# Whole expert blocks of batch 0 run beside batch 1's second pass, from a first list of their own

## The chip, the core and the metric

One core of a Trainium2 chip runs the kernel. The metric is device time in microseconds. TensorE (PE) multiplies matrices and transposes, VectorE (DVE) and ScalarE (ACT) work on tiles, GpSimd (POOL) issues indirect DMAs (gathers and scatters by a list of rows), SyncE (SP) issues plain DMAs. Each engine takes its instructions in order.

## What is computed

A block of a transformer on x of 2 batches x 4096 tokens x 512 features: linear attention, then a mixture of 8 experts of which each token uses 2. Six modulation vectors per batch (`sa, ca, ga, sb, cb, gb`) come from a condition.

```python
h = layernorm(x) * (1 + ca) + sa
q, k, v = split(h @ w_qkv.T); q, k = relu(q), relu(k)      # 16 heads of 32
vk  = einsum('bhen,bhdn->bhed', pad(v, 1), k)              # over all tokens of the batch
att = einsum('bhed,bhdn->bhen', vk, q); att = att[:-1] / (att[-1] + eps)
x = x + ga * (att @ w_proj.T + b_proj)
h = layernorm(x) * (1 + cb) + sb
logits = (h * rsqrt(mean(h*h)) * router_scale / sqrt(512)) @ router_logits
choices = top 2 of logits; weights = softmax over them
out[t] = sum over its 2 experts e: weight * scale[e] * ((gelu(h@Wg[e]) * (h@Wv[e])) @ Wl[e])
x = x + gb * out
```

All tiles are fp32.

## The kernel before, in words

Tokens are handled in blocks of 512 (four tiles of 128), eight per batch.

*First pass* (`prepare`, `first`): layer norm, transposes (`pt`, copied to `xT`), keys (`pk`), queries (`pq`, stored to `q_d`), and the sum of x times k over all tokens (`pa`, added into `acc`). Twelve steps per block, each a `yield`. It also makes sums of the experts' weights (`weight_sums`: `wraw` in, `wnew` out, 24 jobs) for the experts' seven-product scheme.

*Second pass* (`merge`, `attend`, `second_norm`, `route`): `merge` makes the batch's matrix `gm` from `acc` (`pks`, `pvk`, `pgm`). `attend` loads queries (`qi`) and x (`xb`), divides by the denominator (`qk`, `den`), transposes (`pqt`) and projects (`po`, L682). `second_norm` makes `h2`, which goes to DRAM (`h2_d`, `h_d` in the profile), and x so far goes to `out`. `route` takes the top two experts of one or two blocks' tokens, counts ranks with three matmuls into `prk`, and scatters token number and weight to `map_d` in DRAM by `slot` (L887, eight or sixteen scatters). Six steps per block.

*Lists*: when all tokens are routed, `ptot` (L983) sums the counts, and some 40 small VectorE steps make the list of `NBIG` = 25 whole blocks (512 tokens of one expert) and of small ones (128 tokens; `NSURE` = 29 always run, more under an `If`).

*Experts*: a whole block gathers its piece of the map (`mp`), its rows (`xg`) and weights (`wg` twice, `wl`; each a gather of plain quarters and one of the sums), transposes (`px`), and makes two gate matrices and a linear one with seven products each (`seven`, L1200; sums in `part` and `quar`). `put` scales by the batch's `gb` (chosen per token: `sel`, `gsel`) and adds the rows to `out` by a scatter (L1176). A put waits for the one before. Small blocks do the same with plain products (`pgs`, `py`).

The order is written out by generators, and Tile then places the instructions of each engine by their order and readiness. The part around the change:

```python
a, z = firsts(), seconds()
per_block = 3 * NT
for _ in range(NBLK * per_block):
    next(a)
for _ in range((NBLK - 1) * (NT + 2)):
    next(z)
    for _ in range(2):
        next(a, None)
for _ in a:
    pass
for _ in z:
    pass
```

So batch 0's first pass runs alone, then seven blocks of batch 0's second pass go beside batch 1's first, then what is left: batch 0's last block and all of batch 1's second pass, alone. All tiles of these passes lie in pools that are closed before the lists; the experts' pools open after. PSUM (eight banks) is split 2 `ps_t`, 2 `ps_m`, 2 x 2 `ps_w` in the passes, then 2 `pe_t`, 6 `pe_g`. In SBUF, five buffers `big` of 1 MB serve the passes; gate weights `wg` have three buffers, `wl` one.

Of the kernel before, what the change touches and what calls it, by code (L numbers as in the profile page):

```python
# [9 lines left out]
FP = mybir.dt.float32  # L10
# [23 lines left out]
NBIG = (NTOK * TOPK - E * (TB - 1) + TB - 1) // TB  # L34

# [15 lines left out]
def adaln_linear_attention_moe_kernel(  # L51
# [81 lines left out]
    with ExitStack() as st:  # L133
        wp = st.enter_context(tc.tile_pool(name="w", bufs=1))
        wk = st.enter_context(tc.tile_pool(name="wk", bufs=2))
        sm = st.enter_context(tc.tile_pool(name="sm", bufs=2))
        ps_t = st.enter_context(tc.tile_pool(name="ps_t", bufs=2, space=PSUM))
        ps_m = st.enter_context(tc.tile_pool(name="ps_m", bufs=2, space=PSUM))
        ps_w = st.enter_context(tc.tile_pool(name="ps_w", bufs=2, space=PSUM))

        def big(name):
            return wk.tile([P, KC, TB], FP, tag="big", name=name, bufs=5)

        def row(tag, name, bufs):
            return wk.tile([P, C], FP, tag=tag, name=name, bufs=bufs)

        def bank(name):
            return ps_m.tile([P, 512], FP, tag="mm", name=name)

        def two_banks(name):  # L150

            return ps_w.tile([P, 1024], FP, tag="m2", name=name)


        cnd = wp.tile([P, KC, B], FP, tag="cnd", name="cnd")
        nc.sync.dma_start(out=cnd, in_=cond)
        xin = {}

        def load_x(b, i):
            r0 = b * N + i * TB  # L160
            xt = wk.tile([P, NT, C], FP, tag="x", name=f"x_{b}_{i}", bufs=2)
            nc.sync.dma_start(
                out=xt, in_=x[r0 : r0 + TB, :].rearrange("(p t) c -> p t c", t=NT)
            )
            xin[(b, i)] = xt

        def chunks(src):
            return src.rearrange("(k p) n -> p k n", p=P)

        load_x(0, 0)  # L170
        wm_of = {}

        def load_mod(m):
            wm = big(f"wm_{m}")
            nc.sync.dma_start(out=wm, in_=chunks(wmod[:, m * C : (m + 1) * C]))
            wm_of[m] = wm
# [3 lines left out]
        wqk = [  # L180
            wp.tile([P, KC, 2 * C + E], FP, tag=f"wqk{b}", name=f"wqk_{b}") for b in range(B)
        ]
        raw = wqk[1]

        def load_raw(at, c0):
            nc.sync.dma_start(out=raw[:, :, at : at + C], in_=chunks(wqkv[:, c0 : c0 + C]))

        load_mod(0)
        load_mod(1)
        load_raw(0, C)  # L190
        load_mod(4)
        load_raw(C, 0)

        def small_in(name, shape, src):
            t = wp.tile(shape, FP, tag=name, name=name)
            nc.sync.dma_start(out=t, in_=src)
            return t

        rl = small_in("rl", [P, KC, E], rlog)
        rs = small_in("rs", [P, KC], rscale)  # L200
        load_x(0, 1)
        pes_sb = small_in("pes_sb", [P, E], pes.partition_broadcast(P))
        bpc = small_in("bpc", [P, KC], bprojc)
        brow = wk.tile([B, C], FP, tag="sq", name="brow", bufs=1)
        nc.sync.dma_start(out=brow, in_=bproj.partition_broadcast(B))

        nc.vector.tensor_scalar(rs, rs, float(C) ** -0.5, None, ALU.mult)
        nc.vector.tensor_tensor(rl, rl, rs.unsqueeze(2).to_broadcast([P, KC, E]), ALU.mult)


        silu = wp.tile([P, KC, B], FP, tag="silu", name="silu")
        nc.scalar.activation(silu, cnd, AF.Silu)

        modc = wp.tile([P, 5, KC, B], FP, tag="modc", name="modc")

        def mod_columns(m):
            wm = wm_of.pop(m)
            pc = bank(f"pmc_{m}")
            for g in range(KC):
                for k in range(KC):  # L220
                    nc.tensor.matmul(
                        pc[:, g * B : (g + 1) * B],
                        wm[:, k, g * P : (g + 1) * P],
                        silu[:, k, :],
                        start=(k == 0), stop=(k == KC - 1),
                    )
            nc.vector.tensor_scalar(
                modc[:, m].rearrange("p k b -> p (k b)"), pc[:, 0 : KC * B],
                float(m == 1), None, ALU.add,
            )  # L230

        rows_d = dram.tile([7, B * C], FP, tag="rowsd", name="rows_d")

        def keep_row(n, r):
            d = rows_d[n : n + 1, :]
            nc.sync.dma_start(out=d.rearrange("o (b c) -> (o b) c", b=B), in_=r)

        def spread(n, b, dst):

            d = rows_d[n : n + 1, b * C : (b + 1) * C]  # L240
            nc.sync.dma_start(out=dst, in_=d.partition_broadcast(P))

        GA, SB, CB, GB, BG, BK = range(6)

        def mod_row(m):
            wm = wm_of.pop(m)
            pm = bank(f"pm_{m}")
            for k in range(KC):
                nc.tensor.matmul(
                    pm[0:B, :], silu[:, k, :], wm[:, k, :],  # L250
                    start=(k == 0), stop=(k == KC - 1),
                )
            pr = pm[0:B, :]
            r = wk.tile([B, C], FP, tag="qi", name=f"modrow_{m}", bufs=4)
            if m in (2, 5):

                mag = wk.tile([B, C], FP, tag="qi", name=f"mag_{m}", bufs=4)
                nc.scalar.activation(mag, pr, AF.Abs)
                nc.vector.tensor_scalar(mag, mag, 0.25, None, ALU.max)
                nc.vector.tensor_scalar(r, pr, 0.0, 2.0, ALU.is_ge, ALU.mult)  # L260
                nc.vector.scalar_tensor_tensor(r, r, -1.0, mag, ALU.add, ALU.mult)
            else:
                nc.vector.tensor_scalar(r, pr, float(m == 4), None, ALU.add)
            keep_row(m - 2, r)
            if m < 5:
                pc = ps_t.tile([P, 512], FP, tag="tr", name=f"pmt_{m}")
                for k in range(KC):
                    nc.tensor.transpose(
                        pc[:, k * B : (k + 1) * B], r[:, k * P : (k + 1) * P], ident[0:B, 0:B]
                    )  # L270
                nc.vector.tensor_copy(
                    modc[:, m].rearrange("p k b -> p (k b)"), pc[:, 0 : KC * B]
                )
            return r

        def over_parts(cols, name):

            n = cols.shape[2]
            ps = bank(f"ps_{name}")
            for k in range(KC):  # L280
                nc.tensor.matmul(
                    ps[:, 0:n], ones, cols[:, k, :], start=(k == 0), stop=(k == KC - 1)
                )
            return ps[:, 0:n]

        def scaled(b, at):
            for k in range(KC):
                nc.vector.tensor_scalar(
                    wqk[b][:, k, at : at + C], raw[:, k, at : at + C],
                    modc[:, 1, k, b : b + 1], None, ALU.mult,  # L290
                )

        bias = {}

        def bias_row(n):

            pb = bank(f"pb_{n}")
            for k in range(KC):
                nc.tensor.matmul(
                    pb[0:B, :], modc[:, 0, k, :], raw[:, k, n * C : (n + 1) * C],  # L300
                    start=(k == 0), stop=(k == KC - 1),
                )
            r = wk.tile([B, C], FP, tag="qi", name=f"biasrow_{n}", bufs=4)
            nc.scalar.copy(r, pb[0:B, :])
            keep_row(BK + n, r)
            for b in range(B):
                bias[n, b] = wp.tile([P, C], FP, tag=f"bias{n}", name=f"bias{n}_{b}", bufs=2)
                spread(BK + n, b, bias[n, b])

        def over_j(a, n):  # L310
            return a.unsqueeze(3).to_broadcast([P, KC, B, n])

        def over_b(a):
            return a.unsqueeze(2).to_broadcast([P, KC, B, a.shape[2]])


        rlx = wp.tile([P, KC, B, EX], FP, tag="rlx", name="rlx")

        def router_columns():
            nc.vector.tensor_scalar(  # L320
                rlx[:, :, :, E], iota_e[:, 0:1].unsqueeze(2).to_broadcast([P, KC, B]),
# [12 lines left out]
            for b in range(B):  # L334
                nc.vector.tensor_copy(wqk[b][:, :, 2 * C :], rlx[:, :, b, 0:E])
# [45 lines left out]
        def later_rows():  # L381
# [7 lines left out]
            for b in range(B):  # L389
                spread(GB, b, gb[:, b])  # L390
# [1097 lines left out]
```

## Time and profile before

| | us |
|---|---|
| median of 3 runs | 2440.1 |
| lowest, highest | 2439.1, 2448.38 |
| the profiled execution | 2465.07 |
| its span, first to last instruction | 2463.3 |
| first pass of batch 0, `pk` from | 32.0 |
| second pass, `po` from and to | 451.4 to 1109.3 |
| `px` of the first whole block | 1148.8 |
| last product of a whole block | 2438 |

The profile is of one execution. A busy digit is the share of a slice in tenths; the slices are 61.6 us long. A row of the groups gives busy time, mean of one, and the idle time of the engine before it with what ended it. In a row of the table by stage, the columns are busy time and instructions of each engine, the granted TensorE clock, the share of the DMA engines and their rate.

### The profile page before, as it was taken

To read this page: it belongs to the slowest core of one execution; us is meant where nothing else is said; L and a number is where in the kernel's file an instruction comes from. 1 tells how busy PE (TensorE), PEld (TensorE's weight loads), DVE (VectorE), ACT (ScalarE), POOL (GpSimd) and SP (SyncE) were. 2 spreads that over 40 slices of the span, in tenths; PEclk is the share of its full clock that TensorE was granted. 3 is DMA by queue.
4 is the path that set the end of the run, shared out by engine and by line. 5 is a ranking of instruction groups with operands and counts; after the bars stand their busy time and mean duration, and the time that the engine had idled before them with its cause. 6 is when DMAs were issued, how large, how long until landed. Compare 5 with 4: busy or idle time off the path is not lost. (4 is left out here: it accounts for less than half of the span.)

```text
span 2463.3 us, 25420 instructions
## 1 busy us (share of the span) xinstructions
PE 2330.3 (95%) x9446; PEld 1688.4 (69%) x9446; DVE 1469.6 (60%) x2928; ACT 511.8 (21%) x1019; POOL 769.4 (31%) x723
## 2 busy tenths in 40 slices
PE   8999999999899998883899999999999999999996
PEld 4555565666566667662777778777887788877884
DVE  3475656666465648885565655655655566655663
ACT  1121111223232223442111111111111111111110
POOL 0110000000102022255544444444544445444431
PEclk9999999999899999996999999999999999999998
DMA  5685565233434336766777787777777777777763
GB/s 210 258 322 218 218 230 189 73 128 114 101 120 103 137 86 169 198 151 182 246 236 241 215 245 229 234 244 250 209 228 235 246 249 207 233 250 227 243 157 66
DMA packets 111729, 486.22 MB, mean 197 GB/s; under 512 B 18594, under 2 KB 18594, under 8 KB 77939
## 3 DMA queue, kind: packets, MB, share of 16 engines
q0 software_dynamic: 71584, 347.12, 45.3%
q1 hardware_dynamic: 40018, 137.44, 18.3%
q8 instruction: 76, 1.25, 0.2%
q14 instruction: 51, 0.41, 0.1%
HBM read 355.63 MB, written 128.88 MB: 197 GB/s over the span
## 5 line engine op out<-in xcount | busy, mean ns | idle before, releaser
L1200 PE MATMUL p_g<-xT,wg 128*128 128x256 f32 x1600 | 370.7, 380 | 0.0
L1200 PEld LDWEIGHTS p_g<-xT,wg 128*128 128x128 f32 x1600 | 302.5, 190 | 41.7 <-issue 1.9
L887 POOL DMA_INDIRECT map_d<-pair,slot x128 | 134.4, 1050 | 596.2 <-DVE slot L884 548.9
L1200 PE MATMUL p_g<-xS,wg 128*128 128x256 f32 x1200 | 283.6, 379 | 1.4 <-DVE xS L1272 1.4
L682 PE MATMUL po<-gm,qT 128*128 128x265 f32 (+1 forms) x1024 | 247.9, 394 | 13.1 <-issue 6.1
L1200 PEld LDWEIGHTS p_g<-xS,wg 128*128 128x128 f32 x1200 | 227.9, 190 | 32.8 <-DVE xS L1272 1.8
L517 PE MATMUL pq<-wqk,xT 128*128 128x264 f32 (+1 forms) x1024 | 233.0, 387 | 13.0 <-DVE den L658 13.0
L500 PE MATMUL pk<-wqk,xT 128*128 128x512 f32 x512 | 228.3, 593 | 2.8 <-DVE k L505 2.8
L537 PE MATMUL pa<-k,xh 128*128 128x512 f32 x512 | 227.2, 599 | 3.8 <-DVE acc L544 3.8
L517 PEld LDWEIGHTS pq<-wqk,xT 128*128 128x128 f32 x1024 | 196.6, 193 | 49.5 <-issue 18.1
L682 PEld LDWEIGHTS po<-gm,qT 128*128 128x128 f32 x1024 | 193.9, 195 | 50.3 <-issue 10.9
L1176 POOL DMA_INDIRECT out<-y_b,mp x100 | 158.1, 1581 | 180.1 <-DVE y_b L1173 157.3
L1354 PE MATMUL pgs<-wgs,xTs 128*128 128x512 f32 x464 | 205.6, 596 | 0.0
L1200 PE MATMUL p_l<-wl,aT 128*128 128x256 f32 x800 | 193.9, 379 | 0.0
L537 PEld LDWEIGHTS pa<-k,xh 128*128 128x128 f32 x512 | 98.1, 193 | 117.6 <-issue 111.8
L1354 PEld LDWEIGHTS pgs<-wgs,xTs 128*128 128x128 f32 x464 | 88.7, 191 | 111.7 <-issue 110.3
L500 PEld LDWEIGHTS pk<-wqk,xT 128*128 128x128 f32 x512 | 93.5, 190 | 104.4 <-issue 97.8
L1200 PEld LDWEIGHTS p_l<-wl,aT 128*128 128x128 f32 x800 | 147.9, 190 | 18.3 <-issue 0.5
L1113 POOL DMA_INDIRECT xg<-h_d,mp x129 | 131.9, 1022 | 72.7 <-issue 34.0
L1292 ACT ACTIVATE ge<-quar_g 128x512 f32<-128x512 f32 x100 | 62.9, 629 | 409.5 <-DVE quar_g L1208 395.0
L1200 PE MATMUL p_l<-wl,aS 128*128 128x256 f32 x600 | 141.7, 379 | 0.0
L1208 DVE TENSOR_TENSOR quar_g<-part_g,p_g 128x512 f32<-128x512 f32 x150 | 102.7, 685 | 53.6 <-PE p_g L1200 51.9
(267 smaller groups left out, 3017.3 us busy)
## 6 DMA issues: line engine op xcount, KB each, us to landing
x<-in_x SPq DMA_DIRECT2D x16, 1024.0 KB
q_d<-q SPq DMA_DIRECT2D x64, 256.0 KB
qi<-q_d SPq DMA_DIRECT2D x64, 256.0 KB
wraw<-in_wgate POOLq DMA_DIRECT2D x16, 1024.0 KB
xb_d<-x SPq DMA_DIRECT2D x16, 1024.0 KB
wgsum_d<-wnew POOLq DMA_DIRECT2D x16, 1024.0 KB
xb<-xb_d SPq DMA_DIRECT2D x16, 1024.0 KB
out<-xb SPq DMA_DIRECT2D x16, 1024.0 KB
```

What stands on the lines that cost most here:

```text
L500: nc.tensor.matmul(pk, xT[:, k, t * P : (t + 1) * P], w[:, k, 0:C], start=(k == 0), stop=(k == KC - 1),)
L517: nc.tensor.matmul(pq[:, C // 2 + c0 : C // 2 + c1], xT[:, k, t * P : (t + 1) * P], w[:, k, C + c0 : C + c1], start=(k == 0), stop=(k == K ...
L537: nc.tensor.matmul(pa, xh[t][:, g * P : (g + 1) * P], ks[t], start=(t == 0), stop=(t == NT - 1),)
L682: nc.tensor.matmul(po[:, C // 2 - EX + c0 : C // 2 - EX + c1], qT[:, g * P : (g + 1) * P], gm[:, g, c0:c1], start=(g == 0), stop=(g == KC ...
L887: ins = nc.gpsimd.indirect_dma_start(out=map_d, out_offset=IndirectOffsetOnAxis(ap=slot[:, k, t : t + 1], axis=0), in_=pair[:, k, t, :], i ...
L1113: return nc.gpsimd.indirect_dma_start(out=dst, out_offset=None, in_=src, in_offset=IndirectOffsetOnAxis(ap=ids, axis=0))
L1176: ins = nc.gpsimd.indirect_dma_start(out=out, out_offset=IndirectOffsetOnAxis(ap=token(mp, t), axis=0), in_=y, in_offset=None, compute_op= ...
L1200: nc.tensor.matmul(bank[:, c, :], left(s, c, k), rhs[:, k, :], start=(k == 0), stop=(k == KH - 1),)
L1208: nc.vector.tensor_tensor(r, one, two, ALU.add)
L1292: nc.scalar.activation(ge, g, AF.Gelu_apprx_tanh)
L1354: nc.tensor.matmul(p, xT[:, k, :], wg[:, :, quarters[k // KH], k % KH, :], start=(k == 0), stop=(k == KC - 1),)
```

## The change

- `NEARLY` = 9 whole blocks of batch 0's tokens (as many as its 8192 pairs are sure to fill) get a list as soon as batch 0 is routed (`early_lists`), with their nine map gathers at once. Their tokens are all of batch 0, so `put` uses `gb[:, 0]` as it is, and the sources and targets are `h2_d[0:N]` and `out[0:N]`.
- Batch 0's whole second pass now goes beside seven blocks of batch 1's first pass; the eighth follows with the early list.
- Blocks 0 to 7 are cut into steps and run beside batch 1's second pass. PSUM there is 2 transpose banks, one two-bank tile for `po`, 4 product banks.
- After it `late_lists` makes the lists of the other `NLATE` = 16 whole blocks and of the small ones; block 8 is issued after it. Then the 16 blocks run beside the 29 small ones, whose steps end seven steps before the last block does.
- Pools are ordered by how long their tiles live: what only the first pass uses (`at`, `ap`) on one side, what the second pass uses (`bp`, `bk`, `sm`) on the other; the experts' pool `ew` takes the first's place, the small blocks' `sw` the second's, waiting tile by tile. `big` is gone: `xT` has two buffers, weight sums and early loads two (`tmp`), `h2` one, and `wv`, `wo` share those of `xb`. `qo` has two instead of three, `bias` one (read again for batch 1), `wg` two.
- Routing takes blocks two at a time but the last two of each batch (before: the last four of all).

```diff
+NEARLY = (N * TOPK - E * (TB - 1) + TB - 1) // TB
+NLATE = NBIG - NEARLY
...
+        bias[n, b] = ap.tile([P, C], FP, tag=f"bias{n}", name=f"bias{n}_{b}")
+        spread(BK + n, b, bias[n, b])
...
+        alone = n % NBLK >= NBLK - 2
...
+    def early_lists():
+        with ExitStack() as st:
+            mt = pool(st, "mt_early", side="right")
+            n = whole_of(mt, totals("early"), "e")
+            ej, lj, used, _ = first_units(mt, n, NEARLY, "e")
+            place_whole(mt, ej, lj, 0, NEARLY, "e")
+            taken.append(used)
...
+            if early:
+                g = gb[:, 0]
...
-                out=out,
+                out=out[0:N, :] if early else out,
...
-        w = gw.tile([P, NRAW + NSUM, KH, QN], FP, tag="wg", name=f"wg_{j}_{m}", bufs=3)
+        w = ew.tile([P, NRAW + NSUM, KH, QN], FP, tag="wg", name=f"wg_{j}_{m}", bufs=2)
...
+    def block(j):
+
+        more = j + 1 < NBIG
+
+        soon = more and j + 1 != NEARLY
+        if more:
+            fetch_big_rows(j + 1)
+        yield from gate_big(j, 0)
+        if more:
+            fetch_gate(j + 1, 0)
+        yield
+        yield from gate_big(j, 1)
+        if more:
+            fetch_gate(j + 1, 1)
+        if NEARLY <= j + 1 and j + 2 < NBIG:
+            fetch_big_map(j + 2)
+        yield
+        if soon:
+            turn_big(j + 1)
+        yield
+        yield from linear_big(j)
+        if more:
+            fetch_lin(j + 1)
+        if more and not soon:
+            turn_big(j + 1)
+        yield
...
+    def second_passes():
+        yield from seconds(0)
+        early_lists()
+        for j in range(NEARLY):
+            fetch_big_map(j)
...
+    in_turn(a, per_batch - 3 * NT, second_passes(), (NBLK + 1) * (NT + 2) + 1)
...
+    z = seconds(1)
+    next(z)
+    st_a.close()
+    st_p.close()
+    ew = pool(ctx, "ew")
...
+    psum["t"] = pool(st_p, "ps_t2", 2, space=PSUM)
+    psum["w"] = pool(st_p, "ps_w2", 1, space=PSUM)
+    psum["g"] = pool(st_p, "ps_g2", 4, space=PSUM)
...
+    in_turn(blocks(0, NEARLY - 1), STEPS * (NEARLY - 1), z, (NBLK + 1) * (NT + 2) - 1)
+    st_b.close()
+    mt_late = pool(ctx, "mt_late", side="right")
+    late_lists(mt_late)
+    sw = pool(ctx, "sw", side="right")
+    fetch_big_map(NEARLY)
+    fetch_big_map(NEARLY + 1)
+    fetch_small(0)
+    for _ in block(NEARLY - 1):
+        pass
...
+    in_turn(
+        blocks(NEARLY, NBIG), STEPS * NLATE - STEPS // 3, smalls(NSURE), 2 * (NSURE + 1)
+    )
```

`in_turn(one, n, other, m)` takes a step of `one`, then as many of `other` as keep both in proportion, and at the end drains `other`, then `one`.

## The prediction

> **What bounds the kernel now.** I read the page's table of slices first, then busy time by stage, then the timeline of TensorE where the stages meet, then the waits of that stretch.
>
> ```profile
> span 2463.3 us, 25420 instructions
> PE 2330.3 (95%) x9446; PEld 1688.4 (69%) x9446; DVE 1469.6 (60%) x2928; ACT 511.8 (21%) x1019; POOL 769.4 (31%) x723
> PE   8999999999899998883899999999999999999996
> PEclk9999999999899999996999999999999999999998
> ```
>
> TensorE is the bound almost everywhere; one hole lies in slices 16 to 20. By stage:
>
> ```profile
> core 0: us, PE busy (x) PEld busy (x) DVE busy (x) ACT busy (x) POOL busy (x), PEclk, DMA share, GB/s
> 427.00:910.00 483.00, 469.02 (x1749) 310.36 (x1749) 276.90 (x602) 129.56 (x284) 49.88 (x48) 0.98 0.36 110
> 926.70:1112.30 185.60, 154.21 (x723) 126.58 (x721) 159.54 (x500) 86.04 (x194) 68.51 (x64) 0.94 0.70 176
> 1112.30:1148.80 36.50, 2.22 (x11) 2.04 (x12) 22.14 (x107) 5.61 (x13) 23.19 (x29) 0.54 0.48 113
> 1148.80:1200.00 51.20, 41.14 (x162) 30.56 (x162) 18.22 (x28) 9.44 (x15) 26.77 (x29) 0.86 0.82 292
> 1200.00:2441.00 1241.00, 1241.00 (x5367) 964.84 (x5366) 742.35 (x1232) 201.19 (x349) 564.38 (x483) 1.00 0.74 225
> ```
>
> The first row is batch 1's first pass beside batch 0's second. The next is batch 1's second pass alone: VectorE is busy 86% and TensorE starves. Then come routing, lists and first fetches. The last row, the experts, has no TensorE idle time at all.
>
> ```profile
> 824.63 0.60 PE L670 MATMUL pqt<-ident,qi 128*128 128x128 f32 x4
> 825.07 3.69 PE L682 MATMUL po<-gm,qT 128*128 128x265 f32 x16
> 828.59 7.18 PE L517 MATMUL pq<-wqk,xT 128*128 128x256 f32 x32
> 1121.07 0.57 PE L983 MATMUL ptot<-cum,ones 128*128 128x8 f32 x2
> 1148.77 1.39 PE L1263 MATMUL px<-ident,xg 128*128 128x128 f32 x4 [27.12 <-DMA xg<-h_d,mp]
> 1203.70 1.89 PE L1200 MATMUL p_l<-wl,aT 128*128 128x256 f32 x8
> 1205.42 1.89 PE L1200 MATMUL p_l<-wl,aS 128*128 128x256 f32 x8
> ```
>
> Costs at full rate are read from start to start: a second-pass tile is 0.44 us of transposes and 3.52 of `po`; a product of a whole block is 1.73.
>
> **A rule against the row.** By busy time the lone second pass loses 185.6 - 154.2 = 31 us. The Trainium skill (Perfetto Trace Analysis, Identifying the Most-Contended Engine) says that matmul occupancy is a poor measure, because matmuls are pipelined. Here the row does hold stretched matmuls (clock 0.94), so I count: 32 tiles x 3.96 = 126.7, merge 8.2 (`pvk` 3.7, `pgm` 4.5), rank products 3.6, together 138.5. The loss is 47 us, and I take it; the row would give 16 less.
>
> Lost now: 47 alone, 35.5 of the 36.5 until the first rows land, and in 1148.8 to 1200 what remains after 14 products (24.2), 3.5 of transposes and 6.9 of the first small block's `pgs`: 16.6. **Together 99 us.** This is all that covering can win; the matmuls do not change.
>
> **The change, part by part.**
>
> *Whole blocks 0 to 7 beside batch 1's second pass.* One block is 21 products x 1.727 + 16 transposes x 0.11 = 38.0 us; eight are 304. The second pass adds 126.7 and about 3 of rank products: TensorE 434 us. VectorE: the expert stage uses 742.35/1241 x 49.3 = 29.5 us per 49.3 us cycle (start of `py` to start of `py`). Off go 1.16 small blocks of 2.3 us and the block's four `gsel` and `sel` (3.2 by their rows), which early blocks do not make: 23.6. Eight are 189, with the second pass's 159.5 this is 348 us, 80% of 434. DMA: the lone pass used 0.70 x 185.6 / 8 = 16.2 us of all engines per block; a whole block takes 64% of the expert stage's bytes (7.6 MB against 3.7 for a small one), so 0.74 x 1241 x 0.64 / 25 = 23.5. Sum 39.7 of 54.2 us, 73%: the share at which the expert stage has no stall. So TensorE bounds the mixed stage. Its loss can't be read from before; below stands 0 (expert stage), above the 17% of the lone pass's row (31.4/185.6), 74 us. The stage is nearer in VectorE load to the first mixed row (57%, 2.9% idle) than to the lone one: I take 4%, 18 us.
>
> *PSUM and weights.* Four product banks instead of six and one two-bank tile instead of two give VectorE about two products, 3.5 us, of lateness; gate weights have two buffers instead of three. A gather starts when its old half is done and is needed about 26 us of products later, 36 with the second pass's share; 1.84 MB at 225 GB/s fly 8.2 us. Nothing, under that cover; without it 8 us per gather.
>
> *Merge of batch 1.* Today other blocks' `po` lie around `pvk` and `pgm`; idle there is only 1.5 + 2.2 + 0.7 us. Now the first pass has just ended and only block 0's transposes can fill: 6 us (0 to 15, the upper end if row fetches wait for old tiles too).
>
> *Early list, nine map gathers.* Some 20 VectorE steps of about 0.25 us, the scatters of the last route (8 x 1.26 on POOL) and 9 x 1.25 us of gathers, all emitted before the last first-pass block, 43 us of TensorE. Nothing; uncovered about 30.
>
> *Late list beside block 8.* Today the last route's first step starts at 1116.65 and the transposes at 1148.77: 32.1 us. POOL is moved past more: second map, small weights, small map and row, 5 x 1.25, and 3.9 for the map to land before its rows. VectorE shares the time with block 8. So 42 us or more against 36.3 us of products: 10 us lost (0 if the route runs ahead, 25 if block 8's steps go first). What is late next is the first weight gather of block 9, behind those rows.
>
> *Late stage.* Sixteen blocks and 29 small ones: 608 + 29 x 11.2 = 932 us of TensorE. DMA and POOL per us of TensorE stay as now (1.81 small ones per 58 us block instead of 1.16 per 51). Nothing.
>
> *Tail.* Today `py` and its put follow the last whole product: 3.6 us of `py` and a put that waits for the block's four. The small ones now end seven steps earlier: 5 us saved.
>
> *Memory by life.* Weight sums have two buffers of their own, the `h2` tile one, `qo` two, each bias one. Three sums per 43 us block take 3 x (2.7 us of VectorE + 1 MB in and 1 MB out); a q tile is stored in about 4 us and 7 are there. Nothing, with 0 to 15 us kept for the range; at the turn to batch 1 the bias reload stands behind the store of `xb_d` on SP, two `pk` banks (6.9 us) cover it. The one large stall of the first mixed stage, 11.3 us at 637 (VectorE behind a late `qi` load), I leave in.
>
> **Does a busy VectorE slow the gathers?** The rows of the lone pass and of the expert stage:
>
> ```profile
> L887 POOL DMA_INDIRECT map_d<-pair,slot x64: 952/961/1823, 963.2 to 1109.1; - x64
> L1113 POOL DMA_INDIRECT wg<-wgsum_d,wrow x40: 933/937/1013, 1279.0 to 2269.2; - x40
> ```
>
> The Trainium skill (SBUF — State Buffer, A bandwidth-pool intuition that's wrong) tells of a gather's issue of about 620 ns that takes 3100 beside a VectorE copy, since both want one port pair. With VectorE 86% busy the median is 961 ns against 937 at 60%. By the row the 14 issues per block stay near 20 us; by the rule, five times, they would be some 70 us in a 54 us block and POOL the bound. The row decides.
>
> **Sum.** 99 - 18 - 6 - 10 + 5 = 70 us. The profiled execution took 2465.07 us (span 2463.3), 25 more than the median of 2440.1; I take the same 70 off: 2370, and a span near 2393. 0.5%, about what a measurement of this kernel can tell, is 12 us.
>
> **Rivals.**
>
> *Lock-step, 0.20.* VectorE's order is fixed. Today it waits 269/25 = 10.8 us per block for products (its `part` and `quar` rows). If second-pass work can't fill those waits, a block costs 23.6 + 10.8 + 159.5/8 = 54.3 us, exactly TensorE's 54.2; each wait for one then delays the other. Five us more per block are 40: 2410. For it: 76.5 us of VectorE waiting for `qi` loads today, one of which stopped TensorE. Against: the first mixed row hides nearly all of them.
>
> *POOL behind the scatters, 0.08, slower.* POOL is one queue in order, and its scatters wait for `slot`: 548.9 us in all, 22.4 at a time in the lone pass, then 16 x 1.26 = 20 us of issue. Nothing stands behind them now; weight gathers will. Their slack is 36 - 8 = 28 us. If a route's scatters stand in the queue half a mixed block (27 us) ahead of their slots, they hold it for 27 + 20 = 47, TensorE stops for 19, five routes cost 95: 2465. It decides from a hold of 28 us, and is slower than before from some 45. Against: the queue was ordered by what is expected ready, so gathers should go first.
>
> *It does not start early, 0.04.* If the new tiles must wait for all of the first pass's (old stores too), block 0 starts some 15 us late: 2385. Whole-tensor waits between early gathers and `h2` stores would follow program order, no more than a few us per block.
>
> **Numbers.** Forecast 0.68, its own range 2345 to 2395. Range 2335 (mixed stage without loss, late list covered) to 2422 (lock-step with a little more). Faster 0.88 (forecast, most of lock-step, late start), same 0.04, slower 0.08.
>
> **What would show it.** Right: TensorE 9 in nearly all slices, clock 1.0 in the mixed stage, `px` no longer waiting 27 us for rows, VectorE near 80% there, a loss of some 10 us once before the late stage. Wrong: idle TensorE in the mixed stage released by VectorE (lock-step) or by weight gathers behind `map_d` scatters on POOL, or a first pass longer than now.

## The result, and the profile after

The changed kernel took 2409.5 us (median of 4 runs) beside 2441.9 for the one before: ratio 0.986, interval 0.983 to 0.989. It is 32 us faster, where 70 were forecast. The kernel before takes 2442 to 2448 us on some chips and about 2460 on others, and the changed kernel reacts to this more strongly than the one before; so each comparison below is of times on one chip, and the text says what the kernel before took there.

The page of the changed kernel (busy times, then tenths of 40 slices):

```profile
span 2406.8 us, 25334 instructions
PE 2323.5 (97%) x9448; PEld 1683.3 (70%) x9448; DVE 1450.5 (60%) x2915; ACT 536.4 (22%) x1040; POOL 766.8 (32%) x726
PE   7999899999999999999999989999999999999996
PEclk9999999999999999999999999999999999999998
```

The hole of slices 16 to 20 is gone. Busy time by stage: batch 0's first pass, the first overlapped stage, the mixed stage, the change to the late stage, the late stage:

```profile
core 0: us, PE busy (x) PEld busy (x) DVE busy (x) ACT busy (x) POOL busy (x), PEclk, DMA share, GB/s
165.00:425.00 260.00, 240.21 (x764) 141.31 (x763) 147.02 (x254) 43.66 (x91) 20.99 (x39) 0.97 0.64 230
460.50:944.10 483.60, 476.25 (x1818) 319.17 (x1817) 298.63 (x710) 141.51 (x311) 84.06 (x84) 1.00 0.41 128
954.40:1366.20 411.80, 404.86 (x1991) 352.31 (x1989) 326.88 (x715) 146.51 (x274) 172.45 (x149) 1.00 0.68 201
1366.20:1477.60 111.40, 99.97 (x457) 85.21 (x457) 77.70 (x199) 25.80 (x44) 63.30 (x62) 0.94 0.66 203
1477.60:2384.00 906.40, 906.40 (x3739) 667.91 (x3738) 492.86 (x817) 145.51 (x254) 409.00 (x355) 1.00 0.76 238
```

The third row is what was forecast: TensorE 98% busy, VectorE 79%, clock 1.00. The first row is the surprise: the first pass has 20 us of idle TensorE, where the same 260 us of the kernel before read

```profile
165.00:425.00 260.00, 258.19 (x852) 153.95 (x850) 154.56 (x266) 47.60 (x101) 18.06 (x34) 1.00 0.62 222
```

with nearly as many bytes moved. Busy time hides stretched matmuls, so losses below are counted as in the prediction: from start to start, less the cost at full rate. For a pair profiled on one chip (kernel before 2442.7 us, changed kernel 2412.0):

| stage, us lost by TensorE | before | after |
|---|---|---|
| until 165 us | 14.5 | 16.4 |
| rest of batch 0's first pass | 2.1 | 27.2 |
| first overlapped stage | 24.2 | 17.0 |
| merge of batch 1 | 2.5 | 4.4 |
| batch 1's second pass (after: beside blocks 0 to 7) | 26.3 | 12.2 |
| lists and change to the next experts | 52.5 | 17.5 |
| the rest | 2.3 | 1.3 |
| sum | 124.4 | 96.0 |

Sums differ by 28.4, times by 30.7. From the merge to the next experts 47 us less are lost, and 25 of them are paid back in batch 0's first pass, which the change was not thought to touch.

### The profile page after: what moved, and what is told of

It reads as the page before. It is cut to its first block, busy times and chain, and to the rows that moved or that the text cites. A ratio compares the mean times of both kernels' runs of the same rounds, so it can differ in the third digit from the quotient of the medians.

```text
span 2406.8 us, 25334 instructions
## 1 busy us (share of the span) xinstructions
PE 2323.5 (97%) x9448; PEld 1683.3 (70%) x9448; DVE 1450.5 (60%) x2915; ACT 536.4 (22%) x1040; POOL 766.8 (32%) x726
## 3 DMA queue, kind: packets, MB, share of 16 engines
q1 hardware_dynamic: 40018, 137.44, 17.5%
## 5 line engine op out<-in xcount | busy, mean ns | idle before, releaser
L914 POOL DMA_INDIRECT map_d<-pair,slot x128 | 129.1, 1008 | 464.9 <-DVE slot L911 428.2
L542 PE MATMUL pq<-wqk,xT 128*128 128x264 f32 (+1 forms) x1024 | 244.0, 397 | 19.4 <-ACT xl L551 15.1
L709 PE MATMUL po<-gm,qT 128*128 128x265 f32 (+1 forms) x1024 | 237.4, 383 | 5.4 <-DVE den L685 4.6
L1215 POOL DMA_INDIRECT out<-y_b,mp x100 | 163.6, 1636 | 143.7 <-DVE y_b L1212 116.0
L1239 PEld LDWEIGHTS p_l<-wl,aS 128*128 128x128 f32 x600 | 114.5, 192 | 16.8 <-issue 1.4
```

Of the source, the lines that this page charges most:

```text
L542: nc.tensor.matmul(pq[:, C // 2 + c0 : C // 2 + c1], xT[:, k, t * P : (t + 1) * P], w[:, k, C + c0 : C + c1], start=(k == 0), stop=(k == K ...
L709: nc.tensor.matmul(po[:, C // 2 - EX + c0 : C // 2 - EX + c1], qT[:, g * P : (g + 1) * P], gm[:, g, c0:c1], start=(g == 0), stop=(g == KC ...
L914: ins = nc.gpsimd.indirect_dma_start(out=map_d, out_offset=IndirectOffsetOnAxis(ap=slot[:, k, t : t + 1], axis=0), in_=pair[:, k, t, :], i ...
L1215: ins = nc.gpsimd.indirect_dma_start(out=out[0:N, :] if early else out, out_offset=IndirectOffsetOnAxis(ap=token(mp, t), axis=0), in_=y, i ...
L1239: nc.tensor.matmul(bank[:, c, :], left(s, c, k), rhs[:, k, :], start=(k == 0), stop=(k == KH - 1),)
```

## The experiments

Two questions stood after the first profile: whether the 25 us of the first pass come from memory by life, or from the lists or the order; and whether what lies between 2465 (the profile of before) and 2440 (its median) is one odd execution, the profile itself, or something else. Each expectation below has its own letters for its theories.

**The kernel before again**, for the second question. 

> The kernel before, unchanged, profiled once more. Its profile shown with the prediction took 2465 us, 25 more than the median of its other runs, while the changed kernel's profile took what its other runs took. Theory A: that one execution lost some 25 us more than usual, so part of the 99 us that I counted as lost was never there to win in the median; a new profile then spans some 2440 and is shorter in one or two places that can be named (the 11 us stop near 637 us in the first mixed stage, or the lone second pass). Theory B: a profile costs this kernel 25 us each time; then the new span is near 2463 again with the same losses by stage.


It took 2462.6, with the losses of the first profile (144.9 in all against 147.1), while 39 runs of it there had a median of 2459.7. So neither an odd execution nor the cost of a profile: on that chip the kernel is that slow.

**Memory by life alone**, in the kernel before:

```diff
-            return wk.tile([P, KC, TB], FP, tag="big", name=name, bufs=5)
+            tag, bufs = "tmp", 2
+            if name.startswith("xT_"):
+                tag = "xT"
+            elif name.startswith(("h2_", "hk_")) or name == "wm_4":
+                tag, bufs = "h2", 1
+            elif name.startswith(("wv_", "wo_")) or name in ("wm_2", "wm_3"):
+                tag = "xb"
+            return wk.tile([P, KC, TB], FP, tag=tag, name=name, bufs=bufs)
...
-                qt = row("qo", f"q_{b}_{i}_{t}", 3)
+                qt = row("qo", f"q_{b}_{i}_{t}", 2)
```

> The kernel before with the smaller buffers of the change alone: xT its own two, weight sums and early loads two (tmp), h2 one, wv and wo those of xb, qo two instead of three. Order, lists and experts as before. Theory A (the first pass lost its buffers): some 20 us slower than before, 2460, with TensorE idle time between 175 and 400 us as in the changed kernel (29 us there by my count of matmuls against starts, none before). Theory B (that idle time comes from the new order of the changed kernel): within 5 us of before.


2494.5 beside 2459.7, ratio 1.014 (1.012 to 1.016): 35 us slower, where some 20 were expected. The first pass after 165 us lost 28.0 us (0.2 in the kernel before there). Its row:

```profile
165.00:425.00 260.00, 242.57 (x779) 142.91 (x778) 147.49 (x255) 44.13 (x92) 20.99 (x39) 0.97 0.64 229
```

This is the changed kernel's row, to 3 us in every column. What VectorE waits for there, first in the kernel before, then with the memory by life:

```profile
DVE acc L544 <- PE pa L537: 49.0, 24, 2.7
DVE q L523 <- PE pq L517: 34.7, 18, 2.9
DVE bn L469 <- DMA x<-in_x: 1.0, 1, 1.0
```

```profile
DVE q L530 <- DMA q_d<-q: 20.3, 3, 7.6
DVE wnew L453 <- DMA wraw<-in_wgate: 19.3, 9, 3.7
DVE bn L476 <- DMA x<-in_x: 14.1, 5, 4.3
DVE wnew L453 <- DMA wraw<-in_wlin: 10.6, 4, 7.0
```

VectorE waited for TensorE before; now it waits for DMAs as well, and since its order is fixed, TensorE's operands stand behind these waits. Theory A holds: the smaller buffers alone bring the loss. The next three runs ask which buffer it is.

**A third `qo` buffer** in the changed kernel (`ga` moves into the buffers of `qk` to make room):

```diff
-            qt = row("qo", f"q_{b}_{i}_{t}", 2, ap)
+            qt = row("qo", f"q_{b}_{i}_{t}", 3, ap)
...
-        ga = row("ga", f"ga_{b}", 1)
+        ga = row("qk", f"ga_{b}", 2)
```

> The changed kernel with a third buffer for qo, as before (ga takes one of the two qk buffers to make room). In the changed kernel VectorE waits 20 us for stores of q between 175 and 425 us, 13 us of TensorE idle time behind it. Theory A1 (qo is the narrow one): 10 to 15 us faster than the changed kernel, some 2397. Theory A2 (the two buffers of the weight sums are, and the q waits only follow from them): less than 5 us, some 2406.


2462.4 beside 2459.7 for the kernel before; the changed kernel itself, in a later run on this chip, took 2464.0. The waits for `q_d` were gone, but those for `x` (16.9 us) stayed, those for raw weights rose (22.6 to 36.5), and the first pass still lost 24 us. Not `qo`.

**The sums two at a time over 12 blocks**, in the changed kernel:

```diff
-            for _ in range(3 * E // NBLK):
-                next(wsums, None)
-            yield from steps
+            for m, _ in enumerate(steps):
+                if m in (0, 6):
+                    next(wsums, None)
+                yield
```

> The changed kernel with the 24 weight sums spread: two jobs per first-pass block, one before its first step and one before its seventh, over twelve blocks, instead of three at the start of each of eight. Buffers as in the change. Theory A2 (VectorE stops in its order for weights that come late through two buffers): the waits of wnew for wraw (22 us) go, batch 0's first pass is 15 to 25 us shorter, 2390. Theory A1 (qo): 5 us or less, 2405.


2456.5, beside the same 2459.7. Loads of raw weights still followed each other every 13.3 us (12.9 in the changed kernel), and the first pass still lost 24 us: the edit hardly moved the loads, so that it tells little.

**Raw weights into the idle `xb` buffers**:

```diff
-            raw = temp(f"wraw_{n}")
+            raw = temp(f"wraw_{n}", 1)
```

> The changed kernel, with the raw weights of the sums read into the two xb buffers, which nobody uses in batch 0's first pass; the two tmp buffers keep the sums alone. Theory A (the chain load, sum, store through two buffers holds VectorE, and TensorE behind it): the first pass of batch 0 loses under 8 us instead of 21 to 29, 18 to 25 us faster than the changed kernel. Rival (all the loads of this stage queue for the same DMA engines, as the third qo buffer suggests): over 15 us still lost there, the time within 6 us of the changed kernel.


2476.7, against 2463.8 for the changed kernel there: 13 us slower, a miss. More buffers did free the chain: a sum every 8.0 us, all loads issued by 285 us. But until then transfers filled the DMA engines to 84% (the last number but one of this row):

```profile
165.00:290.00 125.00, 104.27 (x325) 60.63 (x326) 84.47 (x147) 19.76 (x41) 16.43 (x31) 0.92 0.84 311
```

In the whole stage VectorE waited 29.7 us for `x`, and the loss stayed 29 us. So more buffers for the sums do not bring the time back.

**The common turn.** In the kernel before, the sums shared five `big` buffers with `xT`, one after the other in turn, so that a sum had to wait for a tile of the block it was in. The timelines of POOL and SP show it: once settled, a raw load is issued 6.9 us after each `x` load, and no other within 12 us of it. In the changed kernel, from 143 to 323 us, two lie around each, 10 to 12 us ahead and 0 to 3 behind, and from 170 to 323 the `x` loads come 50 to 52 us apart and not 43. So, with no byte more:

```diff
-            return a0.tile([P, KC, TB], FP, tag="tmp", name=name, bufs=2)
+            return a0.tile([P, KC, TB], FP, tag="tmp", name=name, bufs=4)
...
-        xT = a0.tile([P, KC, TB], FP, tag="xT", name=f"xT_{b}_{i}", bufs=2)
+        xT = temp(f"xT_{b}_{i}")
```

> The changed kernel with xT back in the pool of the weight sums' buffers, four that turn in common in place of two and two; no byte of memory more. Theory A2 (what the change lost is the common turn, in which a sum had to wait for the block's own tiles, so that its transfers fell between the x loads): the first pass of batch 0 loses under 8 us instead of 26, VectorE waits for x under 5 us there, and the time is 18 to 25 us below the changed kernel. Rival (four buffers are too few for both, the fifth was what mattered): over 15 us still lost, within 8 us of the changed kernel either way.


2399.0 beside a kernel before at 2448.2: ratio 0.980 (0.976 to 0.984). The first pass after 165 us lost 4.5 us, and its `x` loads come 43 to 44 us apart again. The places are not those of the kernel before: one raw load is still 2 to 3 us behind an `x` load, but from 262 us on the next ones lie 14 us or more away on either side. Again, beside the changed kernel itself:

> The changed kernel with the common turn of xT and the sums' buffers, now beside the changed kernel itself. Theory A2: 20 to 25 us below it, whatever the conditions, the loss of batch 0's first pass under 8 us against 20 to 29. Rival (the 2399 came from conditions without disturbed bursts): within 8 us of it.


2444.2 against 2464.0 for the changed kernel and 2461.6 for the one before. The turn is worth 20 us where 20 to 25 were expected; the loss there went from 28.8 to 6.5. Its row of the stage, and three of its waits:

```profile
165.00:425.00 260.00, 254.77 (x849) 152.30 (x849) 150.58 (x263) 48.85 (x103) 19.73 (x37) 1.00 0.63 225
```

```profile
DVE wnew L471 <- DMA wraw<-in_wlin: 26.8, 6, 6.2
DVE bn L494 <- DMA x<-in_x: 4.6, 1, 4.6
DVE q L548 <- DMA q_d<-q: 3.5, 1, 3.5
```

`qo` still has two buffers, and its 20 us of waits are nearly gone. The waits for raw weights are not: 34.3 us in all, about what the run with the third `qo` buffer had (36.5), which lost 24 us; beside that run it is the wait for `x` that is gone (16.9 to 4.6). That separate buffers bring the loss and a common turn takes most of it away is shown. How it acts is not tested by itself: by the place of the transfers, or by their pace, since in the common turn raw loads come every 14.1 us (14.4 in the kernel before, 12.9 in the changed one), about three a block.

**The changed kernel elsewhere.** 

> The changed kernel itself, beside the kernel before at about 2459. Theory (the scatters' bursts cost TensorE 8 to 18 us each in these conditions, in every version): 2455 to 2465, ratio 0.998 to 1.002, and TensorE loses 40 to 50 us in the mixed stage, nearly all of it in the three stretches where 16 map_d scatters follow each other. Rival (the variants tried so far carry costs of their own, the change is worth its 32 us everywhere): about 2427, ratio 0.987, mixed stage losing under 15 us.


2463.8 beside 2462.1: ratio 1.0005 (0.999 to 1.002). The 32 us were gone. A second time, on another chip:

> The changed kernel once more, as the measure for the three below. It took 2409 beside a kernel before at 2442, and 2464 beside one at 2462. If what hampered it there belongs to those conditions, it loses under 15 us in the mixed stage wherever the kernel before takes about 2448 or less, and stands at 2410 to 2430; where the kernel before takes about 2460, it stands at 2460 again.


2464.0 beside 2461.6. The mixed stage lost 57 and 53 us in these two, and 10 in the first profile. Its row in the second:

```profile
972.20:1426.80 454.60, 421.96 (x1991) 359.76 (x1989) 327.38 (x715) 146.97 (x274) 173.25 (x149) 0.95 0.61 182
```

The engines do the same work as in the first profile and take 43 us more for it. TensorE behind a burst of 16 map scatters (a burst: scatters of `route` one after the other on POOL), in that run:

```profile
1146.68 0.81 PE L1239 MATMUL p_g<-xS,wg 128*128 128x256 f32 x3
1148.50 0.59 PE L1239 MATMUL p_g<-xS,wg 128*128 128x256 f32 x2 [1.01 <-issue]
1149.90 0.38 PE L1239 MATMUL p_g<-xS,wg 128*128 128x256 f32 x1 [0.81 <-issue]
1150.62 0.78 PE L1239 MATMUL p_g<-xS,wg 128*128 128x256 f32 x1 [0.34 <-issue]
1152.73 0.58 PE L1239 MATMUL p_g<-xS,wg 128*128 128x256 f32 x1 [1.33 <-issue]
1154.83 2.62 PE L1239 MATMUL p_g<-xT,wg 128*128 128x256 f32 x4 [1.52 <-issue]
```

Matmuls of one product, waiting for nothing that the profile shows, come one by one. The same place in the first profile of the changed kernel:

```profile
1137.72 3.62 PE L1239 MATMUL p_g<-xT,wg 128*128 128x256 f32 x16
1141.17 1.89 PE L1239 MATMUL p_g<-xS,wg 128*128 128x256 f32 x8
1142.90 1.89 PE L1239 MATMUL p_g<-xT,wg 128*128 128x256 f32 x8
```

From a burst's start to 14 us past its end, three bursts of batch 1 cost 12.7, 11.0 and 14.7 us in the one, 1.5, 0.1 and 0.1 in the other. The burst of 8 that follows them cost 0.1 us or less in both.

**Every block routed alone** (8 scatters in a row and not 16), in both kernels:

```diff
-        alone = n % NBLK >= NBLK - 2
+        alone = True
...
-            alone = n >= len(order) - 4
+            alone = True
```

The first two lines are of the changed kernel, the others of the one before.

> The changed kernel with every block routed alone, so that its map scatters go out 8 at a time and not 16. In the runs so far 16 in a row cost TensorE 4 to 15 us, 8 in a row under 1 us unless something else waits there too. Theory B (it is the length of the burst): the stretches behind the scatters of batch 1 lose under 3 us each instead of 10 to 13, and 30 to 40 us fall off the changed kernel, to about 2425. Rival (it is the number of scatters, or their place beside other loads): the same loss in twice as many pieces, and the doubled small steps on VectorE on top, 0 to 10 us slower than the changed kernel.

> The same edit in the kernel before, which lost 9 to 13 us behind each burst of 16 in its lone second pass. Theory B: 25 to 35 us faster than the kernel before; the changed kernel with the edit is then as far below this one as in the first comparison, 15 to 35 us. Rival (the number of scatters): within 8 us of the kernel before, or slower, since VectorE is the busy one in the lone second pass and gets more steps.


2444.5 and 2462.5 beside 2448.2: with the edit the changed kernel is 4 us below the kernel before as it was, and the kernel before loses 14 us by it. (The changed kernel without the edit was not run on this chip.) Behind the bursts of the mixed stage TensorE lost 1.1 us or less, as expected, but the stage lost 32 us all the same, in other places. With the common turn as well:

> Both of these edits in the changed kernel. If both theories hold the gains add: 50 to 60 us below the changed kernel, about 2405 in these conditions, and the fastest of all. If only the bursts matter, as the routed-alone kernel; if neither, within 10 us of the changed kernel.


2432.8, 34 us slower than the common turn alone: the mixed stage lost 27.5 us against 12.8, the first overlapped stage with the merge 35.0 against 21.2. Where bursts cost little, twice as many small steps and bursts only add. As the common turn alone had no long losses behind its bursts there (at most 2.4 in the mixed stage), whether routing alone helps where 16 in a row hurt stays untested; for it speaks that on the two chips of about 2460 the burst of 8 behind the mixed stage's three cost 0.1 us or less.

**Every scatter twice**, with the common turn:

```diff
-        for k in range(TOPK):
+        for k in (0, 1, 0, 1):
```

> The common turn, and each of the 128 map scatters sent twice (the same values to the same rows). If small scatters in long rows hold up all engines' issue: 10 us or more lost behind each of the bursts of batch 1, now 32 and 16 in a row, 40 us or more on the whole. If only POOL and its queue feel them (128 x 1.27 us = 163 us of issue, which other weight gathers stand behind): 8 to 30 us slower, TensorE waiting for gathers and not in issue. If neither: within 5 us.


2579.2 against 2444.2: 135 us slower, far beyond the 40. What TensorE waits for from 950 to 1500 us, longest first:

```profile
PE px L1306 <- ACT xT L1309: 33.3, 5, 31.3
PE po L709 <- issue: 21.0, 13, 3.2
PE p_g L1239 <- issue: 16.3, 15, 1.6
```

Batch 1's bursts of 32 lost 26 to 36 us each, and no weight gather is in this list. The burst of 8 that had cost 0.1 us on this chip is one of 16 now, and cost 11. Behind the first burst of 32 the other engines stand without a wait too:

```profile
1200.20 0.69 DVE L715 TENSOR_TENSOR xb<-po,xb 128x512 f32<-128x512 f32 x1 [17.11 <-issue]
1201.05 0.72 ACT L722 ACTIVATE sv<-xb,lm 128x512 f32<-128x512 f32 x1 [24.09 <-issue]
```

The scatters are the cause. By what way they hold the engines, and why the same bursts cost so much more on one chip than on another, stays open; no run tells whether the recording of the profile has a part in it.

**Without the overlap**: the second pass emitted whole, blocks 0 to 7 behind it.

```diff
-    in_turn(blocks(0, NEARLY - 1), STEPS * (NEARLY - 1), z, (NBLK + 1) * (NT + 2) - 1)
+    for _ in z:
+        pass
+    for _ in blocks(0, NEARLY - 1):
+        pass
```

> The changed kernel without the overlap: the rest of batch 1's second pass is emitted whole, and blocks 0 to 7 behind it; lists, memory and the late stage stay as changed. The overlap's worth by the prediction's own steps is 47 (lone second pass) less 18 (mixed stage), 29 us: 29 us slower than the changed kernel, with VectorE above 80% in a lone second pass again. Rival (the bursts cost the same wherever they lie, so that most of the 47 stays in the mixed stage): within 12 us of the changed kernel.


2482.9 against 2463.8: the overlap is worth 19 us there, between the two forecasts, and VectorE is busy 74% in the lone pass, not above 80. The lone pass lost 72 us, 46 of them behind its three bursts of 16; the mixed stage lost 57, 36 of them behind the same three. Most of what a burst costs stays under the overlap.

**Two blocks beside the late list**, first alone, then with the common turn:

```diff
-    in_turn(blocks(0, NEARLY - 1), STEPS * (NEARLY - 1), z, (NBLK + 1) * (NT + 2) - 1)
+    in_turn(blocks(0, NEARLY - 2), STEPS * (NEARLY - 2), z, (NBLK + 1) * (NT + 2) - 1)
...
-    for _ in block(NEARLY - 1):
+    for _ in blocks(NEARLY - 2, NEARLY):
```

> The changed kernel, with batch 1's second pass spread over blocks 0 to 6, and both blocks 7 and 8 behind it, beside the late list. Theory (one block, 36 us of products, is too short a cover for the late list; 18 us were lost there): 8 to 14 us faster than the changed kernel, px of block 9 no longer waiting for its rows. Rival (the seven blocks carry the same second pass in 54 us less of TensorE, VectorE at 83% there): what is won behind is lost in the mixed stage, 0 to 10 us slower.


2462.3 against 2463.8: no difference.

> The common turn, and batch 1's second pass over blocks 0 to 6 with blocks 7 and 8 beside the late list. If one block is too short a cover (17 us lost there with the common turn): 8 to 14 us below the kernel with the common turn alone. If the mixed stage gives it back, as it did in part without the turn: within 5 us.


2437.0 against 2444.2; the ratios to the kernel before, 0.990 (0.986 to 0.993) and 0.992 (0.990 to 0.995), overlap each other. Block 9's `px` waited 1.5 us for its rows, but the stretch lost 19 us as before, in other waits. Unresolved.

**Both kernels where 2440 is seen.** 

> The kernel before, for a second profile of its lone second pass. If it takes 2440 to 2450 here: what is missing against 2465 is missing behind the four bursts of map scatters of batch 1, so that the lone pass loses 20 to 30 us and not 47, and the burst near 619 us loses nothing. If it takes 2460: the same losses as in the profile of record within 3 us a stage.

> The changed kernel beside it. Where the kernel before takes 2440 to 2450: 2410 to 2430, with under 15 us lost in the mixed stage. Where it takes 2460: 2464 again, 45 to 60 us lost there.


2442.7 and 2412.2 (ratio 0.986, 0.984 to 0.988): the pair of the table above. The lone second pass, from the end of the merge to its last `po`, in the first profile of the kernel before and then in this one:

```profile
936.30:1109.90 173.60, 145.65 (x673) 120.43 (x672) 149.08 (x476) 82.00 (x184) 68.35 (x64) 0.93 0.70 173
```

```profile
933.90:1087.60 153.70, 138.08 (x673) 115.15 (x672) 148.49 (x476) 81.82 (x184) 69.90 (x64) 0.98 0.75 195
```

The same matmuls take 20 us less: 26.3 lost, not 46.2. These are 20 of the 22 us between the two executions (2465.1 and 2442.7). VectorE has the same 149 us of work in both, so these 20 us do not come from more work there; 19 of them lie between a burst's start and 14 us past its end, where three quarters of the pass lie. The 11 us stall of the first overlapped stage did not go with them (10.7 us here), against what was expected.

## Why the prediction was wrong

Its mechanism was right where the kernel before takes 2440: early blocks fill batch 1's second pass, TensorE bounds the mixed stage, there is no lock-step, nothing is held up behind POOL, blocks start without delay. Two steps of its sum failed: the memory, put at nothing, and the 47 us of the lone pass, taken for VectorE's and for wholly coverable. The terms, by the pair of the table:

- *"Together 99 us"* to win: 78.8. The 35.5 and 16.6 stand (52.5 in all); the 47 of the lone pass is 26.3. The count was right for its execution. What failed is its cause and its use: *"VectorE is busy 86% and TensorE starves"* can explain at most 26 of the 47, since the other 20 were not there on another chip, with the same work on VectorE; and with *"I take the same 70 off"* losses of a 2465 us execution were set against a median of 2440, while 20 of the 25 us between lay in the very stage that was being won.
- *Memory by life, "Nothing, with 0 to 15 us kept"*: 25.1 (2.1 to 27.2), the largest miss. The working counted VectorE time, bytes per block and the 4 us of a q store (5.1 here), all of which fit. It did not ask what the shared buffers did to the moment of each transfer, though the text itself named the buffers as separated; with the common turn back, the kernel lost 6.5 us there and not 28.8 on a chip of 2460, and 4.5 on one of 2448. The first pass grew, which was listed as a sign of being wrong.
- *Late list, 10*: 17.5. The changed kernel's first profile has a step that the sum lacked, an iota (a row of numbers, made on POOL) behind 8 scatters, which holds the list's first step on VectorE:

```profile
DVE marksl L119 <- POOL marksl_i L117: 6.8, 1, 6.8
```

Then TensorE waits for block 8's sum on VectorE, and for block 9's rows:

```profile
1421.25 3.02 PE L1239 MATMUL p_g<-xS,wg 128*128 128x256 f32 x8 [3.43 <-DVE quar_g L1247]
1429.15 1.99 PE L1239 MATMUL p_g<-xS,wg 128*128 128x256 f32 x8 [0.77 <-DVE part_g L1247]
1437.64 1.31 PE L1306 MATMUL px<-ident,xg_b 128*128 128x128 f32 x4 [4.77 <-DMA xg_b<-h_d,mp]
```

- *Mixed stage, 18*: 12.2. *Merge, 6*: 1.9 more than before. Both were smaller. *Stall at 637, left in*: it went, and the first overlapped stage lost 7.2 us less; that was luck, no step forecast it. *Tail, 5*: about 3 (1.0 in the table, 2.3 outside).

From 70, then: 21 for the lone pass, 27 for the memory (with 1.9 before 165 us) and 7.5 for the list come off, 2 for the tail; 6 for the mixed stage, 4 for the merge and 7 for the stall come back. That leaves about 30, and 30.7 were measured on that chip.

Where the kernel before takes 2460, another term fails: the mixed stage, put at 18, lost 57 and 53 us, more than the 46 of the lone pass before, so that nothing of the 47 was won and the change was worth nothing (ratio 1.0005). That the 2409.5 us lie within the range of 2335 to 2422 is luck: its upper end was set for the lock-step, which did not come.

The gathers' issue was judged rightly, but on rows of different instructions, a scatter and a gather; and what the prediction called a gather's issue in the rule of the port pair is, on the page that it names, the time of a whole DMA issued by GpSimd. Like with like, the issue of the gather of weight sums took 951 ns (median) in the mixed stage, with VectorE 79% busy, and 941 in the late stage, with 54%.

## What to carry to other kernels

Before buffers are split by life, ask what the shared ones throttled: a common turn also sets when background transfers may start, and giving it back, in the same bytes, was worth 20 us. Losses read from a profile belong to the conditions of that profile; where it stands 1% above the median, find which stage holds the difference before a gain is read from it. And ask what makes a loss before it is counted as one that other work can cover: what holds all engines at once is covered little by more work for them (46 us behind the bursts without the overlap, 36 with it). The common turn makes the change worth its while on both kinds of chip: 2399 beside 2448, 2444 beside 2462.

## What the hardware showed

Scatters of 128 rows of 8 bytes, about 1.26 us of POOL each, can slow the issue of other engines: in the changed kernel 10 to 15 us of TensorE behind each 16 in a row of the mixed stage on two chips, at most 2.6 on others, with the same instructions, and 0.1 or less behind 8 in a row just after. That TensorE does not wait for POOL or for the gathers does not make the scatters free: 128 more of them cost 135 us.
